# Rows for seven feed-forward blocks: turned by a trip to DRAM and VectorE's 32x32 transposes instead of TensorE's

## The chip, the cores and the metric

The kernel runs on one core of a Trainium2 chip. Its engines work side by side, each through its own instructions in order: TensorE (PE; its weight loads are listed apart as PEld), VectorE (DVE), ScalarE (ACT), GpSimd (POOL) and SyncE (SP), which here does nothing but issue transfers. The metric is the device time of one execution, in microseconds (us), as the median of several runs.

## What is computed

The input is 16 sequences of 256 tokens with 256 channels (4096 token rows), in float32. Three layers follow one another, each added to its input and normed:

```python
x = _layernorm(x + _L0_attn_ref(x, ...), axis=-1)
x = _layernorm(x + _L0_xattn_ref(x, ctx_1024, ctx_1024, fside, ...), axis=-1)
x = _layernorm(x + _L0_ffn_ref(x, ...), axis=-1)
```

The first is an attention over fixed keys with squared ReLU, the second a cross attention with 16 heads and a bias worked out from the tokens' fractions. The third, which the change concerns, picks one of 8 experts for each token and adds the expert's low-rank term to a common feed-forward layer:

```python
logits = einsum('bsd,ed->bse', x, gate_W) + gate_b
top1 = argmax(softmax(logits))
base = einsum('bsd,fd->bsf', x, wi_W) + wi_b
lora = einsum('bsr,fr->bsf', einsum('bsd,rd->bsr', x, lora_A[i]), lora_B[i])
expert_out = einsum('bsf,df->bsd', relu(base + lora), wo_W) + wo_b   # kept where top1 == i
```

Both products with x (the gates with lora_A, and wi) sum over the 256 channels, so TensorE needs x with channels on the partitions, while the norm leaves it with tokens on the partitions. That turning is what is changed.

## The kernel before

**Stages.** Stage one (lines 973 to 1053, up to 254 us) runs the first attention over 8 blocks of 512 tokens. Stage two (line 1068) runs 64 groups, numbered n: each of 16 batches has four groups of four heads. The feed-forward layer is laid among them: its eight blocks, `rows_out[0]` to `rows_out[7]`, have 512 tokens each. Block tb is worked on in groups 15 + 8 tb + part with part 0 to 7. Blocks 0 to 5 run wholly among the groups; block 6 ("six") starts in group 63 and ends behind the loop, and block 7 ("seven") runs wholly behind the loop (lines 1217 to 1255).

**One group n, in the order of its engines.** `logits` (line 649) multiplies the group's queries by `kM`, the batch's keys, into four PSUM banks; `maxima` (L664, VectorE) adds the bias and takes the row maxima; `subtract` (L679) is split between GpSimd and VectorE; `turned` (L689, TensorE) and `exps` (L696, ScalarE) follow in the next group, and `attend` (L705) in the one after it. The order is written out by hand: within a manual schedule each engine takes its instructions in the order in which the program lists them.

**What a batch needs through SP.** In each group with n % 4 == 2, in this order: `invert` (L577, L579) sends the inverted sums to DRAM (`rows<-inv`); `keys` (L497 to L513) makes the next batch's keys and copies them into `kM` with eight transfers, four for each half i; `spread` (L587) reads the inverted sums back in eight transfers (`invs<-rows`). Group n + 2 is the first of the next batch: its `logits` need the half i = 0 of `kM`. In group n + 2 `divide` (L594, VectorE) needs `invs`; behind it on VectorE stand the next `qT` (L482) and the maxima of group n + 3. In group n + 1 SP issues the loads of a later batch's context (L438) and fractions (L442).

**A feed-forward block.** In part 7 of the block before (groups 14, 22, ... 62) `root` and `scale` work out the norm's factors, and `rows` (L778) writes the normed rows `x2` (tokens on partitions): for block 0 on GpSimd (L784), late in group 14; for blocks 1 to 6 on ScalarE (recorded at line 245), earlier in their group and ahead of `invert`. In part 0 `turn` (L791) does eight TensorE transposes of 128x128 (recorded at L796) and two ScalarE copies from PSUM (L799) into `xT`. In part 1 `gates` (L811) is the first reader of `xT`, behind that group's `logits` and `attend`. In parts 2 and 3 `inner` (L884) multiplies `wi` by `xT`, into the banks that `maxima` has just read. For block 6 the gates are the first TensorE work of n = 64. Block 7 uses `norm` (L758) and the same `turn`, with the copies on VectorE.

**Buffers and loads.** `x2` comes from three buffers. Transposes take their PSUM tile from a ring of three (`tile_b`). The weights `wi`, the gates and lora_A are loaded once, early (L126 to L137), with channel c * 128 + p on partition p.

Of the kernel before, what the change touches and what calls it, by code (L numbers as in the profile page):

```python
# [9 lines left out]
FP = mybir.dt.float32  # L10
# [4 lines left out]
P = 128  # L15
# [7 lines left out]
def tile_decoder_layer(ctx: ExitStack, tc: tile.TileContext, a: dict, out: bass.AP):  # L23


    nc = tc.nc
    NTOK, C = a["x"].shape
# [3 lines left out]
    CC = C // P  # L31
# [4 lines left out]
    E = a["gate_b"].shape[1]  # L36
# [25 lines left out]
    ident = const.tile([P, P], FP, name="ident")  # L62
# [20 lines left out]
    W = E + ER  # L83
    wq, wk, wv, wo = (const.tile([P, CC, C], FP, name=n) for n in ("wq", "wk", "wv", "wo"))
    wi = const.tile([P, CC, F], FP, name="wi")
    wof = const.tile([P, FC, C], FP, name="wof")
# [14 lines left out]
    gw = const.tile([P, CC, 64], FP, name="gw")  # L101
    nc.gpsimd.memset(gw, 0.0)
    gateb = const.tile([P, 4, E], FP, name="gateb")
    loraB = const.tile([P, F], FP, name="loraB")

    def load_cross():
        load = nc.sync.dma_start
        for t, n in ((vv, "vv"), (wk, "wkT"), (wv, "wvT"), (wq, "wqT")):
            load(out=t, in_=a[n].rearrange("(c p) f -> p c f", p=P))
        for t, n in ((bq, "bq"), (bk, "bk"), (fcol, "frac_cols")):  # L110
            load(out=t, in_=a[n])
        for t, n in (
            (bo, "bo"), (apos, "alpha_pos"), (aneg, "alpha_neg"), (gamma, "gamma"),
            (delta, "delta"),
        ):
            load(out=t, in_=a[n].to_broadcast(list(t.shape)))

        wo_view = a["woT"].rearrange("(o g i d) f -> i g d o f", o=CC, g=4, i=2)
        bv_view = a["bv"].rearrange("x (o g i d) -> i g d (x o)", o=CC, g=4, i=2)
        for i in range(2):  # L120
            for g in range(4):
                rows = slice(64 * i + 16 * g, 64 * i + 16 * g + 16)
                load(out=wo[rows], in_=wo_view[i, g])
                load(out=bvc[rows], in_=bv_view[i, g])

    def load_ffn():  # L126
        load = nc.sync.dma_start
        for t, n in ((wi, "wiT"), (wof, "woffT")):
            load(out=t, in_=a[n].rearrange("(c p) f -> p c f", p=P))
        load(out=wib, in_=a["wib"])  # L130
        load(out=wofb, in_=a["wofb"].to_broadcast([P, C]))
        load(out=gw[:, :, 0:E], in_=a["gateT"].rearrange("(c p) f -> p c f", p=P))
        load(out=gw[:, :, E:W], in_=a["loraAT"].rearrange("(c p) f -> p c f", p=P))
        for j in range(4):
            load(out=gateb[:, j, :], in_=a["gate_b"].to_broadcast([P, E]))
        for g in range(P // ER):
            load(out=loraB[ER * g : ER * g + ER], in_=a["loraB"])  # L137
# [44 lines left out]
    hid = const.tile([P, NT, C], FP, name="hid")  # L182
# [5 lines left out]
    def inv_std(mv, n):  # L188

        return newton(mv, near_root(mv, n), n)  # L190
# [17 lines left out]
    def normed(dst, src, mean, rs):  # L208
        nc.vector.tensor_scalar(dst, src, mean, rs, ALU.subtract, ALU.mult)
# [4 lines left out]
    p2 = ctx.enter_context(tc.tile_pool(name="p2", bufs=2))  # L214
    drams = ctx.enter_context(tc.tile_pool(name="drams", bufs=2, space=bass.MemoryType.DRAM))
# [3 lines left out]
    def tile_x():  # L219
        return px.tile([P, 4, C], FP, tag="x", bufs=3, name="x")  # L220

    def tile_xt():
        return px.tile([P, CC, 512], FP, tag="xt", name="xt")
# [8 lines left out]
    if True:  # L232
# [5 lines left out]
        def scaling_of(mv, rs, n):  # L238
            nm = small.tile([P, n], FP, tag="nm", name="nm")
            nc.vector.scalar_tensor_tensor(nm, mv[:, :, 0], -1.0, rs, ALU.mult, ALU.mult)  # L240
            return rs, nm

        def scaled(dst, src, by, j):
            rs, nm = by
            nc.scalar.activation(  # L245
                dst, src, AF.Identity, bias=nm[:, j : j + 1], scale=rs[:, j : j + 1]
            )

        class Block:
# [3 lines left out]
            def load(self):  # L253
                self.x = tile_x()
                if self.tb:
                    nc.sync.dma_start(out=self.x, in_=x_view[self.tb])
                else:
                    for j in range(4):
                        eng = nc.scalar if j % 2 else nc.sync
                        eng.dma_start(out=self.x[:, j, :], in_=x_view[0, :, j, :])  # L260
# [160 lines left out]
    if True:  # L421

        vaug = []
        for i in range(2):
            t = const.tile([P, 2, NH, 2 * HD], FP, name=f"vaug{i}")
# [319 lines left out]
        def step(piece):  # L745
            if piece:
                next(piece, None)
# [3 lines left out]
    if True:  # L751
        out_view = out.rearrange("(b j p) c -> b p j c", j=4, p=P)

        class Block:
# [2 lines left out]

            def norm(self):  # L758
                rs = inv_std(self.mv, 4)
                self.x2 = tile_x()  # L760
                for j in range(4):
                    normed(
                        self.x2[:, j, :], hid[:, 4 * self.tb + j, :], self.mv[:, j, 0:1],
                        rs[:, j : j + 1],
                    )

            def measure(self, j):
                if j == 0:
# [19 lines left out]
                        continue  # L788
                    scaled(self.x2[:, j, :], hid[:, 4 * self.tb + j, :], self.by, j)

            def turn(self, copy=nc.vector.tensor_copy):  # L791
                self.xT = tile_xt()
                for c in range(CC):
                    ps = tile_b()
                    for j in range(4):
                        nc.tensor.transpose(  # L796
                            ps[:, j * P : (j + 1) * P], self.x2[:, j, c * P : (c + 1) * P], ident
                        )
                    copy(self.xT[:, c, :], ps)  # L799

            def biased(self):

# [146 lines left out]
    with tc.manual_schedule():  # L949
# [18 lines left out]
        by = [None] * (NB + 1)  # L968
# [4 lines left out]
        for tb in range(NB):  # L973
# [23 lines left out]
            if tb + 1 < NB:  # L997
                nxt = rows_in[tb + 1]
# [33 lines left out]
            for m in range(8):  # L1032
                c, n2 = divmod(m, 4)
# [34 lines left out]
        for n in range(N + 2):  # L1068
            now, nxt, last, older = (
                groups[n + d] if 0 <= n + d < N else None for d in (0, 1, -1, -2)  # L1070
            )
            large_piece, small_piece, more = pieces(n)
            tb, part = divmod(n - FIRST, 8)
            ff = rows_out[tb] if 0 <= tb < FUSED or (tb == FUSED and part < 2) else None
            halved = ff and part in (2, 3)

            prep = rows_out[tb + 1] if -1 <= tb < FUSED and part == 7 else None
# [32 lines left out]
            if n == 0:  # L1110
                turn, outs = batches[1].turned(), [rest.turn_out(jj) for jj in range(2)]
                for piece in (turn, early[3], *outs, turn):
                    step(piece)
# [6 lines left out]
            if halved:  # L1120
                for g in range(2):
                    last.turned(g)
                    last.exps(g)
                if part == 2:
                    ff.route()
                now.subtract((nc.gpsimd, nc.vector))
                if part == 2:
                    ff.biased()
                if done:
                    done.ready(newton(done.mv, done.near, 4))  # L1130
                ff.inner(part - 2, range(0, 3))
                if part == 2:
                    ff.turn_um()
                ff.inner(part - 2, range(3, 4))
                ff.lora(part - 2, scalar=(0,))
                for g in range(4):
                    nxt.positive(g)
                older.attend()
            else:


                eager = n in (12, 13, 14)
                for act in ("e0 s0 s1 e1 s2 s3" if eager else "s0 s1 g e0 e1 s2" if ff and part == 0
                            else "s0 s1 g e0 s2 e1 s3").split():
                    g = int(act[1:] or 0)
                    if act == "g":
                        if ff and part == 1 and n < N:
                            ff.keep_gates()
                    elif act[0] == "s":
                        if act == "s3" and n == N:  # L1150
                            older.attend()
                        if nxt:
                            nxt.positive(g)
                    elif last:
                        last.turned(g)
                        last.exps(g)
                if prep and prep.tb:
                    prep.rows()
            if older:
                older.keep()  # L1160
            if n == 0:
# [9 lines left out]

            if inverse:
                inverse.spread()
            if ff and part == 0:
                ff.turn(nc.scalar.copy)
                if nxt:
                    nxt.positive(3)
            divided = batches[b - 2] if og == 0 and b >= 2 else None
            if divided and ff and part != 1:
                divided.divide()  # L1180
# [3 lines left out]
                divided.divide()  # L1184
            if prep and prep.tb == 0:
                prep.rows()
            if done and not halved:
                done.ready(newton(done.mv, done.near, 4))
            if ff and part >= 4:
# [6 lines left out]
                step(large_piece)  # L1196
            step(small_piece)
            step(small_piece)
            if n == N:
                six.route()  # L1200
            for extra in more:
# [2 lines left out]
            if n in measured:  # L1204
                j = measured.index(n)
                row_stats(hid[:, 4 * (NB - 1 - j // 4) + j % 4, :], rest_mv[:, j, :])
            if n in LATE:
                j = LATE.index(n)
                rows_in[NB - 1 - j // 4].norm_out(by[NB], j, j % 4, nc.gpsimd)

            tb, part = divmod(n - FIRST + 4, 8)
# [117 lines left out]
```

## Time and profile before

| | |
|---|---|
| runs shown | 899.75, 899.78 and 899.96 us, median 899.78 |
| the profiled execution | span 898.3 us from first to last instruction; its own total is not listed, and the runs' median is 1.5 us above the span |
| busy | PE 887.4 us (99%), DVE 713.1 (79%), ACT 567.3 (63%), POOL 398.5 (44%) |
| granted TensorE clock | 0.998 of full over the span |
| transfers | 37.01 MB, mean 41 GB/s |
| TensorE transposes of the feed-forward rows (L796) | 64, 272 ns each, overlapping one another |
| the copies behind them (L799) | 14 on ACT, 592 ns each; 2 on DVE, 670 ns each |

A line of the timeline gives the start in us from the beginning of the span, the length, the engine, the line of the program, the operation, the tiles written and read, their shape, how many instructions are merged into the line, and in brackets how long the engine was idle before it and for whom. SPq is SP's queue of transfer issues: the length of such a line is the time in which SP issues, not that in which the bytes move.

### The profile page before, as it was taken

Reading aid. Unit: us, or ns where it says so; the run is one execution under the profiler, and the core shown is the slowest. Engines: PE = TensorE matmul, PEld = TensorE weight load, DVE = VectorE, ACT = ScalarE, POOL = GpSimd, SP = SyncE. Lnnn points to the kernel's source line nnn. Section 1 sums busy time; section 2 is a strip of 40 time slices with the busy share of each in tenths; the row PEclk is TensorE's granted clock in tenths of the full one; section 3 lists DMA queues with packets and bytes.
Section 4 is the critical chain, followed back from the end, with each engine's and each line's share of the span. In section 5 each row is a group of like instructions: output and inputs, shape, how many; then the busy total and the mean of one; then the engine's idle time right before and its main releaser. Section 6 shows DMA issues by size and latency. Waiting matters only on the chain.

```text
span 898.3 us, 19061 instructions
## 1 busy us (share of the span) xinstructions
PE 887.4 (99%) x6940; PEld 560.8 (62%) x6940; DVE 713.1 (79%) x1986; ACT 567.3 (63%) x951; POOL 398.5 (44%) x385
## 2 busy tenths in 40 slices
PE   8999999999999999999999999999999999999997
PEld 4334444444466777577668757766875786586555
DVE  6879899988779999778777877877798787778344
ACT  5766777777787888376656836666684665556111
POOL 1100223422489998435534644563464456344010
PEclk9999999999999999999999999999999999999999
DMA  5501110110001222011111102011110201111001
GB/s 140 154 1 42 53 42 26 30 49 1 14 1 55 70 69 57 14 42 23 34 49 39 47 14 67 20 37 45 43 48 14 66 20 37 43 28 43 23 2 46
DMA packets 44190, 37.01 MB, mean 41 GB/s; under 512 B 14912, under 2 KB 40000, under 8 KB 44096
## 3 DMA queue, kind: packets, MB, share of 16 engines
q1 hardware_dynamic: 43520, 35.52, 14.5%
q8 instruction: 55, 0.90, 0.4%
q14 instruction: 39, 0.32, 0.1%
q10 hardware_dynamic: 576, 0.26, 0.1%
HBM read 21.07 MB, written 6.03 MB: 30 GB/s over the span
## 4 chain that ended last, share of the span: by engine, by line
PE 97%; DVE 1%; ACT 1%; issue 0%; POOL 0%; DVEq 0%; ACTq 0%; POOLq 0%
PE ps_b L689 13%; PE ps_a L339 13%; PE ps_v L358 12%; PE ps_l L884 12%; PE ps_l L649 8%; PE ps_b L914 7%; PE ps_v L705 7%; PE ps_v L914 5%; PE ps_b L601 3%; PE ps_b L497 3%; PE ps_b L471 3%; PE ps_b L519 3%; PE ps_l L896 2%; PE ps_b L811 1%; PE ps_b L458 1%; PE ps_b L796 1%
## 5 line engine op out<-in xcount | busy, mean ns | idle before, releaser
L628 POOL TENSOR_SCALAR neg<-dneg,aneg,delta 128x512 f32<-128x512 f32 x217 | 182.9, 854 | 181.8 <-PE ps_b L689 127.4
L664 DVE CUSTOM_DVE_ANT_0 neg<-ps_l,neg 128x256 f32<-128x256 f32 x512 | 181.5, 420 | 26.5 <-PE ps_l L649 22.6
L640 ACT ACTIVATE ps_l<-dpos,apos_d 128x512 f32<-128x512 f32 x256 | 172.9, 687 | 40.3 <-DVE mx L664 35.6
L696 ACT ACTIVATE pT<-ps_b 128x512 f32<-128x512 f32 x256 | 142.4, 591 | 59.3 <-PE ps_b L689 57.2
L348 DVE TENSOR_TENSOR pr<-pr 128x1024 f32<-128x1024 f32 x128 | 153.9, 1243 | 30.2 <-ACT pr L347 29.8
L347 ACT ACTIVATE pr<-ps_a 128x1024 f32<-128x1024 f32 x128 | 124.9, 1025 | 52.9 <-PE ps_a L339 52.5
L689 PE MATMUL ps_b<-ident,neg 128*128 128x128 f32 x1024 | 138.5, 277 | 2.0 <-ACT pT L696 1.8
L689 PEld LDWEIGHTS ps_b<-ident,neg 128*128 128x128 f32 x1024 | 113.6, 141 | 35.9 <-issue 12.4
L679 POOL TENSOR_TENSOR neg<-neg,mx 128x1024 f32<-128x1024 f32 x65 | 124.2, 1911 | 18.2 <-DVE mx L664 17.0
L339 PE MATMUL ps_a<-xnT,kT 64*64 64x512 f32 x1024 | 124.6, 593 | 1.0 <-ACT xnT L324 0.4
L358 PE MATMUL ps_v<-pr,vv 64*64 64x512 f32 x1024 | 122.7, 589 | 0.0
L884 PE MATMUL ps_l<-xt,wi 128*128 128x512 f32 x248 | 111.5, 595 | 0.0
L679 DVE TENSOR_TENSOR neg<-neg,mx 128x1024 f32<-128x1024 f32 x63 | 99.2, 1575 | 0.6
L413 POOL TENSOR_TENSOR hid<-hid,bo 128x256 f32<-128x256 f32 x32 | 43.7, 1367 | 105.3 <-ACT hid L245 86.5
L358 PEld LDWEIGHTS ps_v<-pr,vv 64*64 64x64 f32 x1024 | 45.2, 133 | 64.4 <-issue 54.5
L339 PEld LDWEIGHTS ps_a<-xnT,kT 64*64 64x64 f32 x1024 | 42.0, 133 | 65.2 <-issue 52.7
L649 PE MATMUL ps_l<-kM,qT 32*128 32x256 f32 x1024 | 75.9, 401 | 0.0
L884 PEld LDWEIGHTS ps_l<-xt,wi 128*128 128x128 f32 x248 | 45.3, 190 | 49.0 <-issue 44.4
L373 POOL TENSOR_TENSOR xt<-xt,half 128x512 f32<-128x512 f32 x15 | 19.1, 1273 | 120.3 <-ACT half L372 120.3
L914 PE MATMUL ps_b<-wof,hT 128*128 128x256 f32 x304 | 68.4, 380 | 0.0
L705 PE MATMUL ps_v<-pT,vaug 128*32 128x256 f32 x1024 | 66.4, 384 | 0.0
L907 DVE TENSOR_SCALAR hT<-ps_l,wib 128x512 f32<-128x512 f32 x43 | 29.8, 746 | 43.9 <-PE ps_l L896 43.9
(131 smaller groups left out, 1087.3 us busy)
## 6 DMA issues: line engine op xcount, KB each, us to landing
cT<-in_ctxT SPq DMA_DIRECT2D x16, 256.0 KB
kM<-keys SPq DMA_DIRECT2D x128, 32.0 KB
v<-raw SPq DMA_DIRECT2D x128, 32.0 KB
invs<-rows SPq DMA_DIRECT2D x128, 32.0 KB
x<-in_x SPq DMA_DIRECT2D x7, 512.0 KB
out<-x SPq DMA_DIRECT2D x7, 512.0 KB
frow<-in_frac SPq DMA_DIRECT2D x16, 128.0 KB
wi<-in_wiT SPq DMA_DIRECT2D x1, 1024.0 KB
```

The lines of the kernel that those rows point to most:

```text
L339: nc.tensor.matmul(sc[64 * k : 64 * k + 64, h, :], lhsT=kT[64 * h : 64 * h + 64, q, hf * P + 64 * k : hf * P + 64 * k + 64], rhs=self.xnT[ ...
L348: nc.vector.tensor_tensor(pr, pr, pr, ALU.mult)
L358: nc.tensor.matmul(self.acc[k][64 * h : 64 * h + 64, :], lhsT=vv[64 * k : 64 * k + 64, hf, 64 * q : 64 * q + 64], rhs=pr[64 * k : 64 * k + ...
L628: nc.gpsimd.tensor_scalar(self.neg[:, g], self.batch.dneg, aneg[:, h : h + 1], delta, ALU.mult, ALU.mult,)
L640: nc.scalar.activation(banks[g], self.batch.dpos.rearrange("p j k -> p (j k)"), AF.Copy, scale=apos_d[:, h : h + 1],)
L649: nc.tensor.matmul(banks[g][:, j * S : (j + 1) * S], lhsT=self.batch.qT[rows, self.o, j * P : (j + 1) * P], rhs=self.batch.kM[rows, self.i ...
L664: nc.vector.tensor_tensor_reduce(out=self.t[:, g, j, :], in0=banks[g][:, j * S : (j + 1) * S], in1=self.neg[:, g, j, :], scale=1.0, scalar ...
L679: eng.tensor_tensor(rows, rows, top.to_broadcast([P, 4, S]), ALU.subtract)
L689: nc.tensor.transpose(ps[:, k * S + j * P : k * S + (j + 1) * P], self.t[:, g, j, k * P : (k + 1) * P], ident,)
L696: nc.scalar.activation(self.pT[:, g, :], self.ps[g], AF.Exp)
L884: nc.tensor.matmul(self.banks[g], lhsT=wi[:, c, f * P : (f + 1) * P], rhs=self.xT[:, c, :], start=(c == 0), stop=False,)
L914: nc.tensor.matmul(ps[:, 0:C], lhsT=self.hT[f][:, j * P : (j + 1) * P], rhs=wof[:, f, :], start=(f == 0), stop=(f == FC - 1),)
```

## The change

The transposes of blocks 0 to 6 go from TensorE to a path through DRAM. Behind `rows`, a new step `regroup` writes `x2` to DRAM in one transfer and reads it back in four, one for each group of 32 partitions, into a tile `z` that has, on partition 32 q + r, for every t the 64 channels from 64 q of token 32 t + r. All five are issued by SP. A new step `turn_blocks` is one VectorE instruction that transposes each 32x32 block of `z` into `xT`. The channels then stand in another order, (q, c, s) instead of (c, p), so `wi`, the gates and lora_A are loaded in that order, in four transfers each instead of one. Block 7 keeps TensorE's transposes; ScalarE writes a second copy of its normed rows with the channels in the new order (`mixed`), which is what is turned.

The calls: `regroup` stands directly behind `rows`, so for blocks 1 to 6 ahead of that group's `invert`, `keys` and `spread`, and for block 0 behind them. `turn_blocks` stands at the end of part 0, where `turn` stood in the middle of it.

```diff
+    def blocked(rows):
+        return rows.rearrange("p (q c s) -> p c q s", q=4, c=CC)
+
+    def load_blocked(t, name):
+        view = a[name].rearrange("(q c s) f -> q s c f", q=4, c=CC)
+        for q in range(4):
+            nc.sync.dma_start(out=t[32 * q : 32 * q + 32], in_=view[q])
...
-        for t, n in ((wi, "wiT"), (wof, "woffT")):
-            load(out=t, in_=a[n].rearrange("(c p) f -> p c f", p=P))
+        load_blocked(wi, "wiT")
+        load(out=wof, in_=a["woffT"].rearrange("(c p) f -> p c f", p=P))
...
-        load(out=gw[:, :, 0:E], in_=a["gateT"].rearrange("(c p) f -> p c f", p=P))
-        load(out=gw[:, :, E:W], in_=a["loraAT"].rearrange("(c p) f -> p c f", p=P))
+        load_blocked(gw[:, :, 0:E], "gateT")
+        load_blocked(gw[:, :, E:W], "loraAT")
...
             def norm(self):
                 rs = inv_std(self.mv, 4)
-                self.x2 = tile_x()
+                by = scaling_of(self.mv, rs, 4)
+                self.x2, self.mixed = tile_x(), tile_x()
                 for j in range(4):
-                    normed(
-                        self.x2[:, j, :], hid[:, 4 * self.tb + j, :], self.mv[:, j, 0:1],
-                        rs[:, j : j + 1],
-                    )
+                    rows = hid[:, 4 * self.tb + j, :]
+                    scaled(
+                        self.mixed[:, j, :].rearrange("p (c q s) -> p c q s", c=CC, q=4),
+                        blocked(rows), by, j,
+                    )
+                    normed(self.x2[:, j, :], rows, self.mv[:, j, 0:1], rs[:, j : j + 1])
...
-            def turn(self, copy=nc.vector.tensor_copy):
+            def regroup(self):
+                away = drams.tile([512, C], FP, tag="rows_ffn", name="away_x")
+                nc.sync.dma_start(
+                    out=away.rearrange("(j p) c -> p j c", p=P), in_=self.x2
+                )
+                self.z = p2.tile([P, 16, 2 * 32], FP, tag="zf", bufs=1, name="z")
+                view = away.rearrange("(t r) (q v) -> q r t v", r=32, q=4)
+                for q in range(4):
+                    nc.sync.dma_start(out=self.z[32 * q : 32 * q + 32], in_=view[q])
+
+            def turn_blocks(self):
+                self.xT = tile_xt()
+                nc.vector.transpose(
+                    self.xT.rearrange("p c (t r) -> p t c r", r=32),
+                    self.z.rearrange("p t (c s) -> p t c s", c=CC),
+                )
...
                 if prep and prep.tb:
                     prep.rows()
+                    prep.regroup()
             if older:
                 older.keep()
...
-            if ff and part == 0:
-                ff.turn(nc.scalar.copy)
-                if nxt:
-                    nxt.positive(3)
+            if ff and part == 0 and nxt:
+                nxt.positive(3)
...
             if prep and prep.tb == 0:
                 prep.rows()
+                prep.regroup()
             if done and not halved:
                 done.ready(newton(done.mv, done.near, 4))
...
             step(small_piece)
             step(small_piece)
+            if ff and part == 0:
+                ff.turn_blocks()
```

More of the change, by code (lines that the diff above doesn't have):

```diff
@@ L789, in rows, with turn @@
                     scaled(self.x2[:, j, :], hid[:, 4 * self.tb + j, :], self.by, j)
-            def turn(self, copy=nc.vector.tensor_copy):
+            def regroup(self):
[13 more added lines that the diff above has]
+                )
+            def turn(self):
                 self.xT = tile_xt()
@@ L796, in turn @@
                         nc.tensor.transpose(
-                            ps[:, j * P : (j + 1) * P], self.x2[:, j, c * P : (c + 1) * P], ident
+                            ps[:, j * P : (j + 1) * P],
+                            self.mixed[:, j, c * P : (c + 1) * P], ident,
                         )
-                    copy(self.xT[:, c, :], ps)
+                    nc.vector.tensor_copy(self.xT[:, c, :], ps)
             def biased(self):
```

## The prediction

> **What bounds the kernel now.** I read the busy shares first, then the chain of work that ended last:
>
> ```profile
> PE 887.4 (99%) x6940; PEld 560.8 (62%) x6940; DVE 713.1 (79%) x1986; ACT 567.3 (63%) x951; POOL 398.5 (44%) x385
> ...
> PE 97%; DVE 1%; ACT 1%; issue 0%; POOL 0%; DVEq 0%; ACTq 0%; POOLq 0%
> ```
>
> TensorE is the bound nearly everywhere: whatever lets it idle is lost, and whatever is taken off it is gained, as long as nothing makes it wait. So I read the timeline around the step, first for block 1 (groups 22 to 24):
>
> ```profile
> 420.70 2.07 ACT L245 ACTIVATE x<-hid,nm,rs 128x256 f32<-128x256 f32 x4
> 420.80 0.33 SPq L579 DMA_DIRECT2D rows<-inv  x1
> ...
> 421.53 5.59 SPq L513 DMA_DIRECT2D kM<-keys  x8
> ...
> 427.17 3.83 SPq L587 DMA_DIRECT2D invs<-rows  x8
> ...
> 427.44 1.01 PEld L796 LDWEIGHTS ps_b<-ident,x 128*128 128x128 f32 x8
> ...
> 428.47 1.22 DVE L679 TENSOR_TENSOR neg<-neg,mx 128x1024 f32<-128x1024 f32 x1
> 428.61 0.86 PEld L689 LDWEIGHTS ps_b<-ident,neg 128*128 128x128 f32 x8
> ...
> 430.07 1.15 PE L649 MATMUL ps_l<-kM,qT 32*128 32x256 f32 x16
> ...
> 432.14 1.08 PE L811 MATMUL ps_b<-xt,gw 128*64 128x256 f32 x8
> ...
> 435.88 0.68 DVE L594 TENSOR_TENSOR oT<-v,invs 128x512 f32<-128x512 f32 x1
> ```
>
> Two things are to be seen. The transposes hold TensorE from 427.44 until the next work at 428.61: 1.17 us, not eight times 272 ns, since they overlap. And SP issues without a pause from 421.5 to 431.0, and its keys are wanted by the logits at 430.07.
>
> **What is removed.** Per block 1.17 us of TensorE and two ScalarE copies of 0.59 us (ScalarE is no bound). Seven blocks: 8.2 us, if nothing waits.
>
> **What is added, and how long the trip takes.** The write has the shape of the output store (L942): 512 KB in 1 KB runs. The transfer view of 459.0 to 462.5, which holds one such store issued at 459.08, shows bytes moving from 460.0 to 461.6; the trace's landing events put its end 2.92 us after the issue. SP takes its list in order, and the reads wait for the write on SP: at 813.70 a small write of 16 KB is issued and the reads behind it start at 815.18, with 1.1 us of waiting on SP put down to that write. For one read's issue I take 0.5 us (L256's 0.38 and L569's 0.64 are the bounds). For issue to landing I take 2.4 us: kM's 32 KB land 1.91 us behind their issue, the 256 KB of L438 2.75 us. So from rows to z: 2.95 + 3 x 0.5 + 2.4 = 6.9 us, and SP is held for 2.95 + 4 x 0.5 = 5 us. Packets of 256 B are in no row. At the byte rate of the store the four reads move in 1.6 us, at its packet rate (512 packets in 1.6 us, z has 2048) in 6.4 us. I take the lower end, since a packet's own time in the trace is 13 ns with 128 B and 46 ns with 1 KB, so it falls with the size, and keep the upper, some 3.8 us later, for the range.
>
> A VectorE transpose is in no row either. The nearest are 128x1024 float32 instructions: 1.24 us (L348) and, with GpSimd beside it, 2.95 us (L679 at 355.04). I take 1.24.
>
> The Trainium skill speaks against the 256-byte runs ("DMA: Bandwidth & Descriptors", Specifications: line rate needs transfers of at least 512 B; Why small descriptors are slow counts 11 cycles where 8 carry data). By it the reads would move in an estimated 2.2 us instead of 1.6, and the sum below would rise by under 4 us; no row here shows it.
>
> **Block 1, worked out.** Rows end at 422.77, so the write is issued at 422.8, the reads from 425.75, z lands at 429.7. VectorE is free at 429.69 (end of L679), `turn_blocks` ends at 430.95, and the gates were at 432.14: z itself comes in time. But behind `regroup` on SP stand `rows<-inv`, the eight kM, the eight invs. The first kM goes from 421.53 to 428.2, the fourth to 428.2 + 3 x 0.635 = 430.1 and lands at 432.0. The first group needs the first four alone: at 301.05 a batch's logits start, when by the same pitch the eighth kM has not landed. Old logits ended on TensorE at 431.15 and could now begin at 428.9; the fourth of sixteen waits for 432.0 and the rest takes 0.6: **1.4 us later than before, the gain already spent**. Then the invs: kM's issue ends at 433.2, the last inv goes at 433.2 + 7 x 0.466 = 436.5 and lands (1.85 us, same shape at 427 to 432) at 438.3. `divide` stood at 435.88. VectorE waits there; behind it stand `qT` (1.0 us) and the maxima of group 25, which started 2.2 us behind `divide`, 0.6 of them spent waiting for TensorE. They now start at 438.3 + 1.6 = 439.9 instead of 438.08: 1.8 us late, and the products of `inner` follow the maxima bank by bank. So 1.8 us, not added to the 1.4. Blocks 2 to 5 have the same pattern (logits 7.3 to 7.8 us behind the rows' end in all five): 5 x 1.8 = **9 us**.
>
> **Block 0.** Here `regroup` is listed behind keys and spread:
>
> ```profile
> 344.00 5.35 SPq L513 DMA_DIRECT2D kM<-keys  x8
> ...
> 349.27 2.90 DVE L679 TENSOR_TENSOR neg<-neg,mx 128x1024 f32<-128x1024 f32 x1
> ...
> 349.40 5.34 SPq L587 DMA_DIRECT2D invs<-rows  x8
> ...
> 352.94 1.08 PE L811 MATMUL ps_b<-xt,gw 128*64 128x256 f32 x8
> ```
>
> SP is free at 354.75, though the rows are done at 346.2. Then 6.9 us: z at 361.7, `xT` at 362.95. VectorE stands still from 352.17, TensorE from 351.8 at the gates, which were at 352.94: **10.0 us**. Nothing covers it, since maxima, exps and the next logits all stand behind those two.
>
> **Block 6.** Rows end at 815.67, z lands at 822.6. VectorE reaches `turn_blocks` only behind the norm of block 5's result, which ends here:
>
> ```profile
> 820.56 1.08 PE L811 MATMUL ps_b<-xt,gw 128*64 128x256 f32 x8
> ...
> 822.32 1.75 DVE L209 TENSOR_SCALAR x<-x,mv,rs 128x256 f32<-128x256 f32 x4
> ```
>
> So `xT` is there at 824.07 + 1.24 = 825.3, and the gates, first on TensorE in group 64, go from 820.56 to 825.3: **4.8 us**. The invs land at about 827.6, `divide` moves from 824.0 to there, less than TensorE's own shift plus the group ahead of `project` (827.56).
>
> **The clock.** Two idles of 11 and 6 us are long. The stage view at the end shows what an idle does:
>
> ```profile
> 893.00:895.00 2.00, 0.00 (x0) 0.00 (x0) 1.27 (x5) 0.50 (x2) 0.00 (x0) 1.00 0.19 66
> 895.00:896.00 1.00, 0.00 (x0) 0.00 (x0) 0.65 (x3) 0.00 (x0) 0.00 (x0) 0.81 0.00 0
> 896.00:897.00 1.00, 0.00 (x0) 0.00 (x0) 0.00 (x0) 0.00 (x0) 0.00 (x0) 0.50 0.36 127
> ```
>
> (After the stretch come its length, the busy times of PE, PEld, DVE, ACT and POOL, PEclk, DMA share and GB/s.) The last matmul ends at 892.9 and the clock halves at about 895.6. At the start the 30 warm-up transposes (L956) take 6.2 us, 0.21 us apart, where L796 has 0.13: about 2.5 us lost in warming. I add 2.5 for each of blocks 0 and 6: **5 us**.
>
> The Trainium skill ("TensorE: Matmul & The Clock Gate", Part 1) has the same halving after an idle window of some 3.4 us, and full rate after some 3.4 us of work; the trace shows 2.7 us and nearly 6. By the page the warming would cost an estimated 1.7 us each time and the sum would be 1.6 us lower.
>
> **What costs nothing.** The nine more weight transfers are issued in stage one, where SP is done at 32.8 us and next wanted at 71.4; should they delay the rows of x behind them, by some 4 us, those still come long before their use. Block 7's ScalarE copy (2.07 us for four, as at L245) starts with the factors at 850.0 and ends at 852.1; the transposes start at 852.8, behind block 6's products. Without that cover it would cost 2 us.
>
> **The sum.** 10.0 + 9 + 4.8 + 5 = 28.8 us (the 8.2 us are inside each term, as every term is measured against the old start of the waiting work). The profiled span becomes 898.3 + 28.8 = 927.1; with the 1.5 us by which the runs' median stands above the span, **928.6 us**, or 3.2% slower.
>
> **The rivals.**
> - *All hidden, faster.* If a waiting transfer does not hold back those behind it on SP, and block 0's z is there by 352, only the removal counts: 899.8 - 8.2 = 891.6. For it: DMA is busy for some 15% only, and z is just in time in blocks 1 to 5. Against it: the wait on SP at 813.70, and block 0, which is late even with an empty queue ahead (346.2 + 6.9 + 1.24 = 354.3). It decides from the point where z and the fourth kM land before 428.9 in block 1. Chance 0.10, and 0.02 for a balance within 0.2% (what a measurement here can tell from no change).
> - *Keys in time, only the ends pay.* If SP's delay is absorbed in blocks 1 to 5, they gain 1.17 us each and blocks 0 and 6 still pay: 10.0 + 4.8 + 5 - 5.9 = 13.9, or 913.7. It needs z's trip to hold SP for some 2 us, not 5; the write's 2.92 us speak against it. Chance 0.18.
> - *Slow pieces.* With 256 B packets at the price of 1 KB packets z is 3.8 us later, and kM behind it lands some 2 us later in five blocks: 3.8 + 5 x 2 + 2.5 = 16 more, 945. A transpose of 2.95 us adds 1.7 in blocks 0 and 6. Beyond 946: chance 0.08.
> - *Not done as said.* The transposes leave TensorE but VectorE becomes the bound: 7 x 1.24 = 8.7 us against 8.2 gained, about 900. VectorE is 79% busy, and idle for 1.68 us just where block 1's transpose falls: contained in the 0.02.
>
> My forecast has 0.62. The range runs from 908 (the second rival without the clock's 5 us) to 946 (slow packets). Slower 0.88, same 0.02, faster 0.10.
>
> **What would show it.** Right: SP's line of kM of group 22 starting some 6.5 us behind the rows' end; logits there waiting for it; VectorE idle for about 9.5 us at `turn_blocks` in group 15; `divide` waiting for invs; PEclk below 1 near 360 and 825; no TensorE transposes of x but eight. Wrong: kM at its old place behind the rows, or gates of block 0 at some 354. What would make the number wrong is above all the reads of 256 B runs and how much of block 0's wait the engines make good.

## The result and the profile after

Measured: **942.38 us** as the median of six runs (937.38 to 945.40) against 899.76 us (899.34 to 899.96) for the kernel before on the same chip; the ratio is 1.0473 [1.0458, 1.0489]. That is 42.6 us more, where 28.8 were forecast; the direction is as forecast, and the time lies inside the range, near its upper end. The profiled execution took 941.3 us, with a span of 939.5.

Lines have moved: logits are now L658, maxima L673, the keys' transfers L522, the spread of the sums L596, `divide` L603, `regroup`'s write L805 and its reads L811, VectorE's transpose L815, the gates L841. The page's busy shares, the granted clock in 40 slices and the chain that ended last:

```profile
PE 902.4 (96%) x6884; PEld 564.9 (60%) x6884; DVE 721.8 (77%) x1994; ACT 563.7 (60%) x941; POOL 403.1 (43%) x385
...
PEclk9999999999999997999999899999989999998999
...
PE 90%; DVE 4%; DMA 2%; ACT 2%; issue 1%; SPq 1%; POOL 0%; DVEq 0%; ACTq 0%; POOLq 0%
```

TensorE has 56 matmuls fewer (7 x 8, the transposes), and yet is busy for 15 us more. The logits account for 9.6 of these (75.9 us before, 85.5 now), since the first ones behind a trip come in pieces, as their keys arrive; and TensorE worked a part of the time at a lower clock. Work of TensorE was 97% of the chain and is 90%; DVE, DMA and SPq have taken its place. What waits for what (us in total, times, longest):

```profile
PE ps_b L841 <- DVE xt L815: 16.6, 2, 10.9
DVE xt L815 <- DMA z<-away_x: 15.2, 6, 9.5
DVE oT L603 <- DMA invs<-rows: 12.0, 7, 3.7
PE ps_l L658 <- DMA kM<-keys: 9.3, 5, 3.5
```

These are the waits that the prediction named: the gates for the turned rows (blocks 0 and 6), VectorE for z, `divide` for the inverted sums, and the first logits behind a trip for the keys, in five blocks. Of the third, one wait of 3.3 us behind the loop was there before. For z the prediction named block 0 alone, with 9.5 us; the other five waits, 5.7 us together, are those of blocks 1 to 5.

The timeline of block 1, whose lines of before were shown in the prediction:

```profile
432.17 2.07 ACT L254 ACTIVATE x<-hid,nm,rs 128x256 f32<-128x256 f32 x4
434.27 0.38 SPq L805 DMA_DIRECT2D away_x<-x  x1
437.20 1.93 SPq L811 DMA_DIRECT2D z<-away_x  x4
439.23 0.43 SPq L588 DMA_DIRECT2D rows<-inv  x1
439.77 5.00 SPq L522 DMA_DIRECT2D kM<-keys  x8
442.20 1.25 DVE L815 STREAM_TRANSPOSE xt<-z 128x1024 f32<-128x1024 f32 x1 [1.04 <-DMA z<-away_x]
442.46 2.42 PE L658 MATMUL ps_l<-kM,qT 32*128 32x256 f32 x16 [1.72 <-DMA kM<-keys]
444.82 3.86 SPq L596 DMA_DIRECT2D invs<-rows  x8
450.17 0.69 DVE L603 TENSOR_TENSOR oT<-v,invs 128x512 f32<-128x512 f32 x1 [0.98 <-DMA invs<-rows]
```

SP issues the write at 434.27 and then nothing until 437.20, when it has landed; the keys, which used to be issued while ScalarE wrote the rows, start 5.5 us behind the rows' end. The logits wait 1.72 us and then take 2.42 instead of 1.15, since they use up the keys as these arrive.

Block 0, where VectorE's idle of 9.50 us and TensorE's of 10.95 are the wait for the trip, and then block 6:

```profile
353.65 0.38 SPq L805 DMA_DIRECT2D away_x<-x  x1
356.60 1.90 SPq L811 DMA_DIRECT2D z<-away_x  x4
361.51 1.25 DVE L815 STREAM_TRANSPOSE xt<-z 128x1024 f32<-128x1024 f32 x1 [9.50 <-DMA z<-away_x]
362.90 1.97 PE L841 MATMUL ps_b<-xt,gw 128*64 128x256 f32 x8 [10.95 <-DVE xt L815]
```

```profile
857.51 1.23 DVE L815 STREAM_TRANSPOSE xt<-z 128x1024 f32<-128x1024 f32 x1
858.89 1.98 PE L841 MATMUL ps_b<-xt,gw 128*64 128x256 f32 x8 [5.66 <-DVE xt L815]
```

The gates take 1.97 and 1.98 us where they took 1.08: the clock is at half. The stage view (length, busy times of PE, PEld, DVE, ACT and POOL, PEclk, DMA share, GB/s) shows that this happens in the middle blocks too. The first pair is block 0, the next two pairs are blocks 1 and 2:

```profile
352.00:363.00 11.00, 0.10 (x2) 0.13 (x4) 1.50 (x5) 0.00 (x0) 2.90 (x4) 0.68 0.58 144
363.00:367.00 4.00, 4.00 (x19) 2.85 (x20) 3.96 (x17) 2.79 (x5) 1.89 (x1) 0.61 0.00 0
440.00:445.00 5.00, 3.28 (x26) 2.06 (x28) 2.81 (x6) 1.84 (x4) 3.68 (x4) 0.96 0.46 79
445.00:449.00 4.00, 4.00 (x30) 1.83 (x25) 3.96 (x17) 1.75 (x3) 1.89 (x1) 0.62 0.29 66
520.00:526.00 6.00, 4.58 (x30) 3.56 (x28) 4.47 (x10) 4.00 (x8) 4.76 (x5) 1.00 0.52 111
526.00:534.00 8.00, 8.00 (x46) 4.47 (x47) 5.25 (x18) 2.30 (x5) 2.88 (x3) 0.57 0.37 89
```

In block 2 TensorE is busy throughout 526 to 534, at 0.57 of its clock. From the start of each group's logits, after minus before: -1.1 us at group 16, 11.5 at 17, 33.5 at 57, 41.2 at the end. So block 0 loses 12.6, blocks 1 to 5 lose 22.0 (3.7, 5.2, 3.7, 6.2, 3.2), block 6 and the tail 7.7. The forecast had 12.5, 9 and 7.3. **The 13 us that were missed all lie in blocks 1 to 5.** (Group 16 starts early since the transposes are already gone there; from group 15, at -0.2, block 0 loses 11.7.)

### The profile page after: what moved, and what is told of

Read it like the earlier page. It is cut to its first block, busy times and chain, and to the rows that moved or that the text cites. A ratio compares the mean times of both kernels' runs of the same rounds, so it can differ in the third digit from the quotient of the medians.

```text
span 939.5 us, 19013 instructions
## 1 busy us (share of the span) xinstructions
PE 902.4 (96%) x6884; PEld 564.9 (60%) x6884; DVE 721.8 (77%) x1994; ACT 563.7 (60%) x941; POOL 403.1 (43%) x385
## 4 chain that ended last, share of the span: by engine, by line
PE 90%; DVE 4%; DMA 2%; ACT 2%; issue 1%; SPq 1%; POOL 0%; DVEq 0%; ACTq 0%; POOLq 0%
PE ps_a L348 12%; PE ps_v L367 12%; PE ps_l L914 11%; PE ps_b L698 11%; PE ps_l L658 8%; PE ps_b L944 7%; PE ps_v L714 6%; PE ps_v L944 4%; PE ps_b L610 3%; PE ps_b L506 3%; PE ps_b L480 3%; PE ps_b L528 2%; PE ps_l L926 2%; DMA kM<-keys 2%; PE ps_b L841 1%; DVE neg L673 1%
## 5 line engine op out<-in xcount | busy, mean ns | idle before, releaser
L637 POOL TENSOR_SCALAR neg<-dneg,aneg,delta 128x512 f32<-128x512 f32 x217 | 186.9, 873 | 189.5 <-PE ps_b L698 115.9
L673 DVE CUSTOM_DVE_ANT_0 neg<-ps_l,neg 128x256 f32<-128x256 f32 x512 | 181.4, 420 | 29.7 <-PE ps_l L658 26.6
L357 DVE TENSOR_TENSOR pr<-pr 128x1024 f32<-128x1024 f32 x128 | 153.8, 1243 | 30.3 <-ACT pr L356 29.8
L698 PEld LDWEIGHTS ps_b<-ident,neg 128*128 128x128 f32 x1024 | 115.9, 142 | 37.1 <-issue 16.0
L658 PE MATMUL ps_l<-kM,qT 32*128 32x256 f32 x1024 | 85.5, 412 | 9.3 <-DMA kM<-keys 9.3
L714 PE MATMUL ps_v<-pT,vaug 128*32 128x256 f32 x1024 | 71.5, 407 | 0.0
L658 PEld LDWEIGHTS ps_l<-kM,qT 32*128 32x128 f32 x1024 | 53.1, 188 | 26.5 <-issue 11.4
```

The source lines that it names most:

```text
L357: nc.vector.tensor_tensor(pr, pr, pr, ALU.mult)
L637: nc.gpsimd.tensor_scalar(self.neg[:, g], self.batch.dneg, aneg[:, h : h + 1], delta, ALU.mult, ALU.mult,)
L658: nc.tensor.matmul(banks[g][:, j * S : (j + 1) * S], lhsT=self.batch.qT[rows, self.o, j * P : (j + 1) * P], rhs=self.batch.kM[rows, self.i ...
L673: nc.vector.tensor_tensor_reduce(out=self.t[:, g, j, :], in0=banks[g][:, j * S : (j + 1) * S], in1=self.neg[:, g, j, :], scale=1.0, scalar ...
L698: nc.tensor.transpose(ps[:, k * S + j * P : k * S + (j + 1) * P], self.t[:, g, j, k * P : (k + 1) * P], ident,)
```

## The experiments

Theory A: the trip holds up SP's list, so keys and sums come late; and each idle of TensorE this makes costs clock besides the wait. Its rivals stand with the runs. All medians are of four runs, against 899.6 to 899.9 us of the kernel before on the same chip.

| run | us | ratio to before |
|---|---|---|
| no trip, all by TensorE (e1_mixed) | 911.50 | 1.0133 [1.0116, 1.0150] |
| trip in block 0 alone (e2_block0) | 922.02 | 1.0251 [1.0236, 1.0266] |
| the same, z ahead of the sums (e8_early0) | 917.23 | 1.0197 [1.0182, 1.0212] |
| trip in blocks 1 to 5 alone (e3_mid) | 928.62 | 1.0314 [1.0290, 1.0337] |
| before, plus a trip nobody reads (e4_unread) | 916.44 | 1.0184 [1.0168, 1.0199] |
| the same, list of SP split (e12_unread_split) | 903.47 | 1.0042 [1.0027, 1.0057] |
| after, idles filled, too much (e5_filled) | 944.49 | 1.0502 [1.0486, 1.0517] |
| after, idles filled (e9_refilled) | 929.49 | 1.0333 [1.0316, 1.0350] |
| blocks 1 to 5, list of SP split (e6_split) | 914.50 | 1.0158 [1.0133, 1.0183] |
| ... gates later (e7_split_lg) | 918.53 | 1.0212 [1.0194, 1.0230] |
| ... transpose a group later (e10_later) | 916.78 | 1.0185 [1.0165, 1.0206] |
| ... transpose last, gates in part 2 (e11_last) | 909.81 | 1.0117 [1.0100, 1.0133] |

### Which blocks lose

The weights stay in the new channel order, so a block that does not take the trip is turned by TensorE from rows that ScalarE writes a second time, as block 7 does.

```diff
 prep.rows()
-prep.regroup()
+prep.regroup() if prep.tb in DRAM else prep.mix()   # mix: four more ScalarE copies, into z's tile
```

DRAM is empty in the first run, (0,) in the second, (1, 2, 3, 4, 5) in the third.

> No trip and no VectorE transpose: all eight blocks are turned by TensorE, from rows that ScalarE writes a second time with the channels in the new order (four copies more per block, some 2.1 us of ScalarE); the weights stay in the new channel order. Theory A (SP's list is held by the trip, and each idle of TensorE then costs clock as well): none of the 42.6 us is left but what the ScalarE copies cost; 900 to 904. Rival B (the new channel order, its nine more weight loads or the changed buffers cost something by themselves): more than 905, and the late start shows in stage one.

> Only block 0 takes the trip; blocks 1 to 6 are turned by TensorE from a second ScalarE copy. Theory A: block 0 keeps its whole loss, about 11.7 us as the logits' starts of the changed kernel show it, so 11 to 13 us above the kernel without any trip. Rival C (a delay of one block is made good in the groups behind it, and the losses of the changed kernel come from several trips following one another): under 6 us.

> Only blocks 1 to 5 take the trip; blocks 0 and 6 are turned by TensorE. Theory A: each of the five loses as in the changed kernel, 3.2 to 6.2 us, together 20 to 24 us above the kernel without any trip. Rival D (the waits alone, as the prediction had them, 1.8 us each; the rest of the 22 us is an echo of block 0's delay): 8 to 11 us.

The first came out above what theory A said, 911.5, where rival B had it. But stage one is not late (-0.9 us at group 15), so weights and order cost nothing that shows; each of blocks 0 to 6 adds 1.2 to 2.1 us, in the group behind its copies. ScalarE shows why:

```profile
421.62 2.07 ACT L255 ACTIVATE x<-hid,nm,rs 128x256 f32<-128x256 f32 x4
423.58 2.07 ACT L255 ACTIVATE z<-hid,nm,rs 128x256 f32<-128x256 f32 x4
425.55 1.06 ACT L706 ACTIVATE pT<-ps_b 128x512 f32<-128x512 f32 x2
```

The exps, which everything waits for, stand behind the second copy; in the kernel before they start at 422.66, behind the first. This is a cost of my control and not of the change; ScalarE, 60% busy, had no room at that place. In later runs the copies stand at the end of the group, and blocks 0 and 6 then cost about 0.9 us together.

In the second run group 17 is 14.7 us later than group 16, more than in the changed kernel (12.6; the half clock lasts a window longer), and the 13.7 us are still there at every later group, only increased by the copies' 1.2 to 1.7 per block behind it. Rival C falls: no delay is made good. In the third run blocks 1 to 5 lose 5.1, 3.7, 5.1, 6.6 and 5.3, together 25.8 us, without block 0's delay; theory A had 20 to 24. The half clock takes nine stretches of 3.4 us there, against seven in the changed kernel. Rival D, which had my prediction's 9 us, falls.

### What of it is SP's list

```diff
 # e4_unread, on the kernel before
 prep.rows()
+if prep.tb < FUSED: prep.regroup()        # z is read by nobody; TensorE turns as before
 # e12_unread_split instead: the write behind the 2nd of the eight kM, the reads behind the 6th
+behind_key.update({1: prep.send, 5: prep.fetch})
```

> The kernel before, with the write and the four reads of blocks 1 to 5 issued where the changed kernel issues them, but nobody reads what they bring: TensorE turns all rows as before, channels in the old order. Theory A: SP is held all the same, so the keys and the inverted sums come some 6 us late; the old transposes fill 1.2 us of each idle, so the loss is 9 to 22 us in all. Rival E (what costs is that z or the VectorE transpose is late, not that SP is held): within 2 us of the kernel before.

> The kernel before with the unread trip of blocks 1 to 5, as in the earlier unread run (916.4), but with the write behind the second transfer of the keys and the reads behind the sixth. The transfers are the same, only their place on SP's list differs. Theory A (SP standing still for the write is what costs in the unread run): 899 to 902. Rival J (five more transfers and 5.2 MB on the queues cost by themselves): 910 or more.

The waits between 415 and 780 us, first of the unread trip, then of the same transfers with SP's list split:

```profile
DVE oT L594 <- DMA invs<-rows: 8.5, 5, 2.2
...
PE ps_l L649 <- DMA kM<-keys: 3.8, 6, 0.9
PE ps_b L689 <- DVE qT L482: 3.4, 3, 1.6
```

```profile
DVE oT L595 <- DMA invs<-rows: 1.7, 2, 0.8
...
PE ps_b L690 <- DVE qT L482: 0.6, 1, 0.6
```

With nobody waiting for z, the five trips still cost 15.0 us in the spans' stages (16.8 in the medians): rival E falls. With the same five transfers issued at places where SP need not stand still, 3.6 us are left (3.7 in the medians): rival J falls, with a small remainder, among it the sums that still come late (1.7 us of waiting). Theory A had 899 to 902, so a little more is left than it said. Some 11 to 13 us, then, are SP standing for the write with keys and sums behind it. And in the profiled execution of the unread run the clock stays at full all through the loop, with TensorE idle for at most 0.9 us ahead of the logits, since the old transposes fill 1.2 us of each gap. Its other three executions took 1.7 to 3.5 us longer, at a mean clock of 0.994 to 0.997 instead of 0.998, so the same waits can cost some clock too; the 15.0 us are the waits alone.

### What of it is the clock

```diff
+def fill(count):                          # products that nobody reads
+    ps = tile_b()
+    for _ in range(count):
+        nc.tensor.matmul(ps, lhsT=ident, rhs=wof[:, 0:2, :]..., start=True, stop=True)
 # ahead of block 0's gates, of the logits of part 1 in blocks 1 to 5, of block 6's gates:
+fill(24), fill(4), fill(12)               # e5_filled;   fill(12), fill(2), fill(6)   # e9_refilled
```

> The changed kernel with products on TensorE that nobody reads, laid into its idles (0.45 us each): 24 ahead of block 0's gates, 4 ahead of the first logits behind each trip of blocks 1 to 5, 12 ahead of block 6's gates. No wait is shortened. Theory A (the idles cost clock besides the wait): the stretches at half clock go, which last 40 us in the changed kernel and in which TensorE works for about half; 6 to 14 us below the changed kernel, 928 to 936. Rival F (the waits alone make the loss): no gain, 941 to 946.

> As the filled run, with half the products, since each turned out to hold TensorE for 0.86 us and not 0.45: 12 ahead of block 0's gates (10.3 us against an idle of 10.95), 2 ahead of the first logits in blocks 1 to 5 (1.7 us against 1.1 to 3.5), 6 ahead of block 6's gates (5.2 against 5.66). Theory A (clock besides the waits): block 0 some 10.2, blocks 1 to 5 together 11 to 13, block 6 and the tail 6; 925 to 931. Rival F (the waits alone make the loss): within 3 us of the changed kernel, 939 to 945.

The first missed, at a time that rival F had named: a float32 product is two instructions here and holds TensorE for 0.86 us, so block 0's filling took 20 us against an idle of 11 and cost what the clock gave. With half of it the time is 929.49, 12.9 us below the changed kernel, inside what theory A said. The same stretches of that run:

```profile
352.00:363.00 11.00, 10.50 (x24) 4.41 (x24) 0.91 (x2) 0.00 (x0) 2.90 (x4) 1.00 0.61 145
363.00:367.00 4.00, 3.25 (x21) 2.47 (x22) 3.96 (x18) 2.88 (x6) 1.89 (x1) 1.00 0.00 0
440.00:445.00 5.00, 4.82 (x40) 2.37 (x37) 2.90 (x7) 1.44 (x4) 3.64 (x4) 1.00 0.42 70
445.00:449.00 4.00, 4.00 (x33) 2.94 (x26) 3.65 (x13) 3.74 (x7) 1.89 (x1) 1.00 0.23 63
520.00:526.00 6.00, 6.00 (x40) 3.72 (x42) 3.35 (x4) 2.52 (x5) 4.24 (x5) 1.00 0.59 106
526.00:534.00 8.00, 7.99 (x75) 5.87 (x74) 6.68 (x25) 6.36 (x12) 4.08 (x4) 1.00 0.36 92
```

PEclk is 1.00 in every row, and TensorE does work for nobody on top. SP stands for the write as long as before, but for block 4: 2.96 us there instead of the changed kernel's 4.93, so up to 2.0 of the 12.9 us are not the clock's. By stages, changed kernel and filled one: block 0 12.6 and 12.1, blocks 1 to 5 22.0 and 12.2, block 6 and the tail 7.7 and 5.0. Theory A had 10.2 for block 0, so there the clock cost less than it said. Rival F falls. Useless work that makes a kernel faster by over 10 us shows that the clock was part of the price.

### Block 0's place on SP's list

```diff
 # group 14, on e2_block0
-inverse.spread()
 ...
 prep.regroup()
+inverse.spread()
```

> Only block 0 takes the trip, and its write and reads stand ahead of the eight transfers of the inverted sums on SP, not behind them. Theory A (block 0's loss is the trip's length and its place on SP's list): z lands 5 us sooner, so some 4 to 6 us below the run in which block 0 alone takes the trip (922.0), 916 to 918. Rival H (the inverted sums, now 5 us later, take the place of z as the last to come): within 2 us of that run.

917.23: as theory A said. SP's write goes out at 348.06 instead of 354.28, block 0 loses 9.6 us instead of 14.7, and the later sums cost nothing that shows.

### Can the trip be hidden?

```diff
 # e6_split: blocks 1 to 5 take the trip, blocks 0 and 6 TensorE with late ScalarE copies
+behind_key.update({1: prep.send, 5: prep.fetch})     # instead of regroup behind rows
 # e7_split_lg, in addition: gates behind the first two groups of transposes of part 1
 # e10_later, instead: turn_blocks in part 1 behind subtract, gates at the end of part 1
 # e11_last, instead: turn_blocks at the end of part 1, in part 2 gates and inner(0, range(0, 1)) ahead of route
```

> Blocks 1 to 5 take the trip, but SP's list is laid so that nobody waits on it: the write goes behind the second transfer of the keys, the reads behind the sixth, when the write has landed. Blocks 0 and 6 are turned by TensorE from a second ScalarE copy, laid at the end of the group. Theory A (what SP's wait for the write holds back makes the loss): the keys are in time, the inverted sums some 2 us later than in the kernel before, against 3 us of slack, z some 0.5 us late; with 1.17 us less of TensorE per block 896 to 904. Rival G (the reads of 256 B runs slow the keys and the inverted sums wherever they stand, or VectorE's transpose becomes the bound): 908 or more.

> As the run with the split list, and the gates of blocks 1 to 5 stand behind the first two groups of transposes of their step instead of ahead of them, so that z may land some 3 us later. If a late z is what is left in the run with the split list, this one is 1 to 3 us faster than it; if inverted sums or VectorE are, it is within 1 us of it.

> The run with the split list, and VectorE's transpose of blocks 1 to 5 one group later, behind its half of subtract, with the gates at the end of that group. Theory A, as it stands after the split list (SP no longer holds keys and sums back; what is left there is VectorE standing in front of its transpose until z lands, 10 us behind the rows, with the maxima queued behind it): the wait goes, each of the five blocks keeps 0.8 to 1.2 us of gain, blocks 0 and 6 cost some 0.9 us of ScalarE: 894 to 899. Rival I (VectorE has no room for five transposes of 1.24 us, or the reads slow other transfers): 902 or more.

> The run with the split list; in blocks 1 to 5 VectorE's transpose stands at the end of part 1, behind divide and qT, and the gates in part 2 behind the first two groups of transposes, with one piece of inner between them and route, so that nothing that TensorE or the maxima need stands behind the transpose. Theory A (what is left after the split list is work queued behind VectorE's transpose, first because z is late, then because qT comes 1.24 us later and holds the PSUM tile that the gates take): nearly all of the 15 us go; 897 to 904, of which some 0.9 is the ScalarE copy in blocks 0 and 6. Rival I (the trip's reads slow other transfers, or VectorE has no room wherever it stands): 908 or more.

None of the four came out as theory A or the late z said. In the first, keys and sums are in time, so the half of rival G that blames the reads falls: against the kernel before, the logits are 0.6 us early at group 23 and 1.4 at group 24, and these 0.8 us are the gain from the transposes. But then, with SP's write and reads in the first two lines:

```profile
423.22 0.53 SPq L821 DMA_DIRECT2D away_x<-x  x1
...
426.62 2.13 SPq L830 DMA_DIRECT2D z<-away_x  x4
...
432.26 1.25 DVE L834 STREAM_TRANSPOSE xt<-z 128x1024 f32<-128x1024 f32 x1 [3.15 <-DMA z<-away_x]
...
433.65 1.08 PE L860 MATMUL ps_b<-xt,gw 128*64 128x256 f32 x8 [2.88 <-DVE xt L834]
```

z lands at 432.24 by the trace's landing events, 10 us behind the rows; the expectation had it only some 0.5 us late. The fourth read takes 3.97 us from issue to landing. VectorE stands in front of its transpose, and the maxima, which need no z, stand behind it. Moving the gates alone, away from that wait, halved what they wait (12.4 to 6.1 us), but VectorE waits for z as before (13.7 and 12.6), and nothing was gained (918.5; why it is 4.0 us more is not shown). With the transpose moved behind the maxima z was no longer waited for, but the gates now were:

```profile
517.62 1.23 DVE L834 STREAM_TRANSPOSE xt<-z 128x1024 f32<-128x1024 f32 x1
518.79 0.84 DVE L605 TENSOR_TENSOR oT<-v,invs 128x512 f32<-128x512 f32 x1
519.55 0.98 DVE L492 TENSOR_SCALAR qT<-ps_b,qscale,bq_s 128x256 f32<-128x256 f32 x2
520.59 1.98 PE L860 MATMUL ps_b<-xt,gw 128*64 128x256 f32 x8 [3.33 <-DVE qT L492]
```

They take the PSUM tile out of the ring of three that qT still reads, and qT comes later by the transpose. With the transpose behind qT and the gates in part 2 the time is 909.8, the least with a trip that is used: groups 24 and 25 start 0.8 and 0.9 us earlier each, and group 25 gives 2.9 back, 1.1 of them the gates that moved into it. No version with the trip beats the kernel before. The time lies where rival I had it, and VectorE's lack of room would fit: its stretch from the maxima of group 24 to those of group 25 had 0.62 us to spare before, against the transpose's 1.24. That this is the cause is not shown. What the remaining 10 us of the last run consist of is not settled: the gates still wait for the transpose (4.9 us in three), two waits for sums (2.7 us) and one stretch of half clock (3.4 us) are among them.

## Why the prediction was near, and where it failed

- **Block 0, 10.0 us**: right, with some luck. The gates were forecast for 363.0 and start at 362.90; VectorE's idle was to be 9.5 and is 9.50. Two errors cancel: the trip takes 7.7 us and not 6.9 (the write lands after 2.94, as forecast; the last read after 3.30, not 2.4), and the write goes out at 353.65, 1.1 us earlier. That the place on SP's list decides is shown by e8_early0.
- **Blocks 1 to 5, waits of 5 x 1.8 = 9 us**: right in mechanism, and 9 is the least that the runs allow. In block 1 the fourth of the keys lands 9.35 us behind the rows (9.2 forecast; 928.9 stands there for 428.9), in block 4 only after 11.36, since SP stands 4.9 us for the write there. The unread run, whose profile has no lost clock, loses 15.0 with the old transposes in place; less 5 x 1.17 for their removal is 9.1. But TensorE waits another 3.8 us for the keys behind those transposes, so their removal need not save all of that, and the filled run loses 12.2. The waits lie between, with up to 2.0 us on top in the changed kernel's profile for the longer pause in block 4. z, forecast to come in time, kept VectorE waiting for 0.4 to 2.7 us in each block; that cost nothing that shows, since behind the transpose the maxima still stood 1.2 to 2.0 us for the logits.
- **Block 6, 4.8 us**: right. Gates at 858.89 less the 33.5 us that had gathered by then is 825.4, against 825.3.
- **The clock, "I add 2.5 for each of blocks 0 and 6: 5 us"**: this step failed. By the filled run it is 0.5 in block 0, 9.8 in blocks 1 to 5 and 2.7 at block 6, 13.0 in all. (In block 0 z is 0.6 us later in the filled run, so it may be 1.1 there.) Block 4's longer pause takes up to 2.0 off, so in the middle blocks 7.8 at least; the 22.0 less the 2.0 and 9.1 of waits leaves 10.9 at most. That is still more than all that was forecast for the clock. I took it that only the long idles cost clock, and had no row for a short one. In block 0 VectorE's maxima run without a pause behind the idle, so most of the half clock seems to be hidden there.
- **What was to cost nothing** does cost nothing: the weights' extra transfers (-0.2 us at group 15) and block 7's second copy (7.7 us at the end are 4.8, the clock's 2.7 and 0.2). VectorE's transpose takes 1.23 to 1.25 us, as estimated.
- **The rivals**: "all hidden" and "keys in time" fall with SP's pause in every block: 2.9 to 3.1 us from the write's issue to the first read's, 4.9 in block 4. "Not done as said", about 900, falls with them. "Slow pieces" named 945, near the measured time, but for another reason: the trip is 0.8 us longer than estimated, not 3.8, and the transposes are as short as estimated.

The Trainium skill ("TensorE: Matmul & The Clock Gate", Part 1) lets the clock fall to half after an idle window of about 3.4 us that runs freely. The changed kernel's half-clock stretches last 3.4, 6.8 and 10.2 us, multiples of that window, and their starts lie whole multiples of 3.413 us apart, from 355.90 to 857.65. But the idles ahead of the logits are 1.72, 1.38, 1.56, 3.46 and 1.14 us, all but one well under a window, and each went with a half-clock stretch: it seems that a window only has to be partly idle. How much of it is not shown, and the idle's length alone does not decide: in the profile of e6_split idles of 2.88 and 1.81 us ahead of the gates passed at full clock, and one of 1.88 did not. The page's 3.4 us at half, an estimated 1.7 us of loss each, would make an estimated 12 us of the seven such windows in the five middle blocks, a little above the 7.8 to 10.9 that the runs leave.

## What to carry to other kernels

A transfer that had to wait for another on the same queue held up everyone behind it on that list: price the pause first (here 2.9 us or more, with keys and sums behind it), and look for a place on the list where the wait has run out by itself. When a step leaves the bounding engine, ask what gap its work had been filling: gaps that grew from some 0.7 to 1.7 us here went with a loss of clock about as large as the waiting. And a wait moved to an in-order engine that feeds the bound, as VectorE here, was not hidden by that engine's idle time, some 22% on average.

## What the runs showed of the hardware

- TensorE's granted clock fell to 0.5 for 3.4 or 6.8 us after idles of 1.1 to 3.5 us followed by logits that ran as their keys arrived (2.4 to 3.6 us instead of 1.15). In the profile of the unread run, with idles of at most 0.9 us ahead of the logits and one of 1.6 elsewhere, it did not.
- Within each profiled execution the starts of the half-clock stretches lie whole multiples of 3.413 us apart.
- Four reads of 128 KB in 256 B runs, issued 0.5 us apart by one queue, landed 2.41, 2.91, 3.19 and 3.30 us after their issue in block 0; with the keys' transfers among them up to 4.6 (4.59 in e6_split, 4.63 in e11_last).
- A VectorE transpose of 128x1024 float32 in 32x32 blocks takes 1.23 to 1.25 us, as much as the two-input operation of that size at L357 (1.24).
